# RWKV layer, tree feed-forward, attention and mixture of experts in one kernel: one product of the rwkv chunk moved from VectorE to ScalarE and GpSimd, with a new order of work

## The chip, the cores and the metric

The kernel runs on one core of a Trainium2 chip. The metric is the device time in microseconds (us). The engines are named as the profile names them: PE (TensorE matmuls, PEld its weight loads), DVE (VectorE), ACT (ScalarE), POOL (GpSimd) and SP (SyncE, which only issues transfers here).

## The reference

Sixteen sequences of 512 positions with 128 features pass through two layers. Each step is followed by a layer normalization of the input plus the step's result. Cut to what matters:

```
x = ln(x + rwkv_block(x))      # layer 0, attention place
x = ln(x + tree_ffn(x))        # layer 0, feed-forward: 8 levels of gates, 256 leaves
x = ln(x + rope_attention(x))  # layer 1: 16 heads of 8, causal softmax
x = ln(x + moe(x))             # layer 1: 16 experts, the 2 best gated, 2 shared

# inside rwkv_block, after two norms and the mixes with the shifted input:
k = exp(min(xk @ Wk, 60)); v = xv @ Wv; r = xr @ Wr; kv = k * v
# over time, for each of 512 channels:  wk_t = first*k_t + s_t,  s_{t+1} = k_t + decay*s_t
#                                       wkv_t = first*kv_t + u_t, u_{t+1} = kv_t + decay*u_t
rwkv = sigmoid(r) * (wkv / (wk + 1e-8))
x = x + rwkv @ Wo
# channel mix:
kv = silu(xk @ cWk) @ cWv
x = x + sigmoid(xr @ cWr) + kv
```

The kernel writes sigmoid(r) as (1 + tanh(r/2)) / 2, with the half in the weights. So each rwkv chunk contains a product with 1 + t, where t = tanh(r/2). The silu of the channel mix is likewise ph * (1 + tanh(ph/2)), up to the same half.

## The kernel before

**A planner at build time.** The kernel is written as Python generators ("pieces"), one for each strand of work. The class `Plan` (L66) runs them on modelled engine times while the program is built, and so decides in which order each engine's instructions are issued. On the chip each engine runs its own list strictly in this order; semaphores do the rest. A piece that wants an engine which is busy in the plan queues for it, and the queue is ordered by the time of asking plus the piece's *slack* for that engine. The slacks are the dictionaries `S_FRONT`, `S_RWKV`, `S_GREATEST`, `S_WEIGHTED`, `S_SUMS`, `S_ENDS`, `S_GATE` and `S_EXPERTS` (L46 and on): a smaller number goes first. All instructions pass through the helper class `Engine` (L209), so nearly every row of the profile carries the line L219, and rows are told apart by their tiles.

**The pieces.** For each of the 16 sequences (`b`) there is a `front` (L547): two norms, the mixes `xk`, `xr`, `xv`, four rwkv chunks of 128 channels (`rwkv(c)`, L597), the channel mix with four `hidden(c)` (L666), the tree (`gates`, `lp`), and the queries and keys with rotary positions, split into three bf16 parts each (`parts`, L779) and sent to DRAM (`there`). A front starts when the one before has summed its rwkv product (`p<-rw`), the one before that has passed its channel mix, and the plan's clock has reached PERIOD * b - LEAD. Beside the fronts run pieces that loop over all sequences: `operands` (loads of `qop`, `kop`), `greatest` (scores `sc` and their maxima `nmx`), `weighted` (scores `st` and their exponentials `ew`), `sums` (`o`), `ends` (output of the attention, norm, `u`), `gating` (`gaug`, the gates broadcast through DRAM into `gb`), `by_gate` (`us` = `u` times a gate, on POOL) and `experts` (`acc`, sixteen matmuls on the `us`). So about three sequences are in work at once.

**Slots.** PSUM has eight banks (`BANKS`) that all matmul results share; `SCORES` says how many of them score tiles may hold at once. Two rwkv chunks may be open at a time (`chunks`), two tiles `t` of the channel mix (`halves`), three `us`.

**The rwkv chunk.** Per chunk, 128 x 512 each: DVE clamps `pk` to `k`; ACT takes exp in place and t = tanh(pr/2); DVE makes `kv`; ACT makes `fk` = first*k + eps; DVE scans `sk` and then `skv`; POOL adds `fk` to `sk`. Then

```python
            W.scalar_tensor_tensor(skv, kv, first[:, c:c + 1], skv, ALU.mult, ALU.add)
            W.scalar_tensor_tensor(skv, t, 1.0, skv, ALU.add, ALU.mult)
            yield
            V.reciprocal(sk, sk)
            yield
            G.tensor_tensor(rw[:, c, :], skv, sk, ALU.mult)
```

`V` and `W` are DVE (`W` with a plan cost that counts a busy POOL), `G` is POOL, `act` is ACT, `mm` is PE.

Of the kernel before, what the change touches and what calls it, by code (L numbers as in the profile page):

```python
# [11 lines left out]
AF = mybir.ActivationFunctionType  # L12
ALU = mybir.AluOpType
# [26 lines left out]

HAND_OVER = 0.2
BANKS = 8
SCORES = 4
PERIOD = 107.0

S_FRONT = {"PE": -6.0, "V": -6.0, "A": 0.0, "G": 10.0}  # L46
S_RWKV = {"PE": -10.0, "V": 15.0, "A": 10.0, "G": 6.0}
S_GREATEST = {"PE": -15.0, "V": -6.0, "A": -6.0, "G": 20.0}
S_WEIGHTED = {"PE": -3.0, "A": -6.0}
S_SUMS = {"PE": 6.0}  # L50
S_ENDS = {"PE": 3.0, "V": -3.0, "A": 30.0, "G": 50.0}
S_GATE = {"V": 6.0, "G": 15.0}
S_EXPERTS = {"PE": 20.0}
FREE = {}
LEAD = 60.0
RWKV_PACE = 5.0
EXPERT_PACE = 0.0
MAX_PACE = 0.0
EXP_PACE = 0.0
# [198 lines left out]
def rwkv_tree_attn_moe(ctx: ExitStack, tc: tile.TileContext, a: dict, out: bass.AP):  # L258
# [16 lines left out]
    plan, table = Plan(tc), [None]  # L275

    def scalar_us(op, out, x, f=None, *_):
        us, wanted = 0.2 + 0.00078 * columns(out), {AF.Ln: "ln", AF.Tanh: "tanh"}.get(f, table[0])
        if wanted != table[0]:
# [4 lines left out]
    mm, tr, act, copy = (Engine(plan, "PE", nc.tensor, tensor_us).matmul, Engine(plan, "PE", nc.tensor, tensor_us).transpose,  # L284
                         Engine(plan, "A", nc.scalar, scalar_us).activation, Engine(plan, "A", nc.scalar, scalar_us).copy)
# [5 lines left out]
    W = Engine(plan, "V", nc.vector, beside)  # L291
    V, G = Engine(plan, "V", nc.vector, vector_us), Engine(plan, "G", nc.gpsimd, pool_us)
    banks, scores, chunks, sets = Banks(plan, BANKS), Slots(plan, SCORES), Slots(plan, 2), Slots(plan, OPERANDS)
    e_slots, us_slots, gb_slots = Slots(plan, 2), Slots(plan, 3), Slots(plan, 2)
    halves, norms = Slots(plan, 2), Slots(plan, 1)
    shifts = Slots(plan, 1)
    held, happened = {}, {}

    def event(*key):
        return happened.setdefault(key, Event(plan))  # L300
# [12 lines left out]
    def fixed(name, shape, dtype=F32):  # L313
        return const.tile(shape, dtype, tag=name, name=name)
# [27 lines left out]

    V.memset(mean_w, 1.0 / D)
    V.tensor_tensor(centre, ident, mean_w, ALU.subtract)
    eps = fixed("eps", [128, 4])
    V.memset(eps[:, 0:1], LN_EPS)
    V.memset(eps[:, 1:2], RMS_EPS)
    V.memset(eps[:, 2:3], K_EPS)

    V.memset(eps[:, 3:4], LN_EPS * RMS_EPS)  # L350
    ln_eps, rms_eps, k_eps, z_eps = (eps[:, i:i + 1] for i in range(4))

    def centred(w, scale):

# [147 lines left out]
    def bank(name, shape=(128, 512), dtype=F32):  # L502
        i = yield banks
        p = ps.tile(list(shape), dtype, tag=f"b{i}", name=name)
        held[id(p)] = p, i
        return p

    def give(p):
        banks.put(held.pop(id(p))[1])
# [3 lines left out]
    def t512(tag):  # L513
        return (p2 if tag in twice else pp).tile([128, T], F32, tag=tag, name=tag)
# [32 lines left out]
    def front(b, keep):  # L547

        if b:
            yield event("summed", b - 1)  # L550
            if b > 1:
                yield event("mixed", b - 2)
            yield max(0.0, PERIOD * b - LEAD - plan.now)
        sq, rr = f"sq{b % 2}", f"r{b % 2}"
# [42 lines left out]
        def rwkv(c):  # L597
            chunk = yield chunks
            cs = slice(c * 128, (c + 1) * 128)
            pk = yield from bank("pk")  # L600
            mm(pk, tm_k[:, cs], xk, start=True, stop=True)
            yield
            k = t512(f"k{chunk}")
            V.tensor_scalar(k, pk, K_CLAMP, None, ALU.min)
            give(pk)
            pr = yield from bank("pr")
            mm(pr, tm_r[:, cs], xr, start=True, stop=True)
            yield
            act(k, k, AF.Exp)
            t = t512(f"t{chunk}")  # L610
            act(t, pr, AF.Tanh, scale=0.5)
            give(pr)
            pv = yield from bank("pvv")
            mm(pv, tm_v[:, cs], xv, start=True, stop=True)
            yield
            kv = t512(f"kv{chunk}")
            V.tensor_tensor(kv, k, pv, ALU.mult)
            give(pv)
            fk = t512(f"fk{chunk}")
            act(fk, k, AF.Identity, bias=k_eps, scale=first[:, c:c + 1])  # L620
            dec = decay[:, c:c + 1].to_broadcast([128, T - 1])
            sk = t512(f"sk{chunk}")
            skv = t512(f"skv{chunk}")
            G.memset(sk[:, 0:1], 0.0)
            G.memset(skv[:, 0:1], 0.0)
            W.tensor_tensor_scan(sk[:, 1:T], dec, k[:, 0:T - 1], 0.0, ALU.mult, ALU.add)
            yield
            G.tensor_tensor(sk, fk, sk, ALU.add)
            W.tensor_tensor_scan(skv[:, 1:T], dec, kv[:, 0:T - 1], 0.0, ALU.mult, ALU.add)

            W.scalar_tensor_tensor(skv, kv, first[:, c:c + 1], skv, ALU.mult, ALU.add)
            W.scalar_tensor_tensor(skv, t, 1.0, skv, ALU.add, ALU.mult)
            yield
            V.reciprocal(sk, sk)
            yield
            G.tensor_tensor(rw[:, c, :], skv, sk, ALU.mult)
            chunks.put(chunk)
            event("rw", b, c).set()

        for c in range(NC4):  # L640
            plan.start(plan.now + RWKV_PACE * c, rwkv(c), S_RWKV)
        yield event("outputs")
# [21 lines left out]
        hid = pp.tile([128, NC4, T], F32, tag="four", name="hid")  # L664

        def hidden(c):  # L666
            ph = yield from bank("ph")
            mm(ph, cm_k[:, c * 128:(c + 1) * 128], xk, start=True, stop=True)
            yield
            slot = yield halves  # L670
            t = t512(f"t{slot}")
            act(t, ph, AF.Tanh, scale=0.5)
            yield
            V.scalar_tensor_tensor(hid[:, c, :], t, 1.0, ph, ALU.add, ALU.mult)
            give(ph)
            halves.put(slot)
            event("hid", b, c).set()

        for c in range(NC4):
            plan.start(plan.now + 1.2 * c, hidden(c), S_FRONT)  # L680
        pr = yield from bank("pr2")
        mm(pr, cm_r, xr, start=True, stop=True)
        yield
        t = xr
# [91 lines left out]
            G.tensor_tensor(rot[:, i, :], rot[:, i, :], rs, ALU.add)  # L776
        event("rot", b).set()
        yield
        parts = pp.tile([128, PARTS, 2, T], BF16, tag="parts", name="parts")  # L779
        copy(parts[:, 0], rot)  # L780
        yield
# [10 lines left out]
        there = dram.tile([2, PARTS, 128, T], BF16, tag="there", name="there")  # L792
        for n in range(2):
            nc.sync.dma_start(out=there[n].rearrange("a p t -> p a t"), in_=parts[:, :, n, :])
        keep["z"], keep["xa"], keep["there"] = z, xa, there
        yield 4.0
        event("there", b).set()
# [67 lines left out]
    def values(b, keep):  # L865
        if b:
            yield event("o", b - 1, NG - 1)
        pv = yield from bank("pvt")
        for t in range(NT):
            mm(pv[:, t * 128:(t + 1) * 128], keep["xa"][:, t * 128:(t + 1) * 128], w_qkv[:, 4, :], start=True, stop=True)  # L870
        yield
        copy(vheads[:, :, :, 0:DH], pv.rearrange("p (t h d) -> p t h d", t=NT, d=DH))
        give(pv)
        event("values", b).set()

    def weighted():

        for b in range(B):
            for g in range(NG):
                yield event("max", b, g)  # L880
                if g == 0:
                    plan.start(plan.now, values(b, kept[b]), S_ENDS)
                n, qo, ko = kept[b]["ops", g]
# [174 lines left out]
    def experts():  # L1058

        for b in range(B):  # L1060
# [13 lines left out]
            yield  # L1074
            plan.start(plan.now, output(b, acc), S_ENDS)

    def output(b, acc):
        slot = yield norms
        r = yield from normed(acc, "sqb", "rb")
        V.tensor_tensor(r, r, acc, ALU.mult)  # L1080
        give(acc)
        event("out", b).set()
        yield
        pt = yield from bank("pout")
        for t in range(NT):
            tr(pt[:, t * 128:(t + 1) * 128], r[:, t * 128:(t + 1) * 128], ident)
        yield
        o = t512("sqb")
        copy(o, pt)
        give(pt)  # L1090
        nc.sync.dma_start(out=out[b].rearrange("(t p) d -> p t d", p=128), in_=o.rearrange("p (t d) -> p t d", d=D))
        norms.put(slot)

    kept = {b: {} for b in range(B)}
    for b in range(B):
        plan.start(0.0, front(b, kept[b]), S_FRONT)
    for piece, slack in ((prepare_mixes, FREE), (prepare_tree, FREE), (prepare_attention, FREE), (prepare_experts, FREE), (operands, FREE),
                         (greatest, S_GREATEST), (weighted, S_WEIGHTED), (sums, S_SUMS), (ends, S_ENDS), (gating, S_ENDS),
                         (by_gate, S_GATE), (experts, S_EXPERTS)):
        plan.start(0.0, piece(), slack)  # L1100
# [54 lines left out]
```

## Time and profile before

| what | us |
|---|---|
| median of 3 runs | 1921.01 (1915.64 to 1925.85) |
| the profiled execution, its own time | 1919.29 |
| its span on the engines | 1917.5 |

Busy in that span: PE 1710.9 us, DVE 1515.0, ACT 1073.4, POOL 833.9. A row of the profile's groups gives line, engine, operation, tiles as out<-in, shapes, number, busy us and mean ns, and then the idle time just before these instructions with what ended it. A row of a tile's view gives min/median/max ns in place of the mean. "The chain of waits" follows the work that ended last back to its start, and shares the span out among what it passes through.

The first `xk` of the sequences begin at 24, 98, 182 and 271 us, and from there to the sixteenth at 1595 us once in 110.3 us.

### The profile page before, as it was taken

The numbers are of one execution on the slowest core, as the hardware profiler recorded it, in microseconds if no ns is written. First come the engines' busy times: TensorE is split into PE (matmuls) and PEld (weight loads), VectorE is DVE, ScalarE is ACT, GpSimd is POOL, SyncE is SP. The second block draws the span as 40 slices with busy tenths as digits, with TensorE's granted clock in tenths as the row PEclk, the third lists the DMA queues.
The fourth block names the chain that finished last, engine by engine and source line by source line (L and its number), as shares of the span: only waits on it lengthen the run. The fifth ranks groups of instructions, "written<-read, shape, count | busy, mean of one in ns | idle before, by whom it ended". The sixth has DMA issues, their size and how long they took to land.

```text
span 1917.5 us, 25366 instructions
## 1 busy us (share of the span) xinstructions
PE 1710.9 (89%) x8659; PEld 795.3 (41%) x8750; DVE 1515.0 (79%) x2255; ACT 1073.4 (56%) x1806; POOL 833.9 (43%) x963
## 2 busy tenths in 40 slices
PE   5556799999999999999999998989999999999995
PEld 2122344444444444444444444434444444444442
DVE  7595989797797979788887979969797988966433
ACT  3334567556466565656666564746556466565541
POOL 1223233543353546354553544436454454535353
PEclk8687999999999999999999999999999999999998
DMA  3001011312213122121312222122222212133333
GB/s 99 1 6 54 19 44 31 98 52 60 81 41 98 65 81 81 56 89 38 114 54 82 79 78 82 41 75 70 85 71 82 73 62 84 44 88 105 112 115 101
DMA packets 61969, 133.78 MB, mean 70 GB/s; under 512 B 11708, under 2 KB 32974, under 8 KB 61585
## 3 DMA queue, kind: packets, MB, share of 16 engines
q1 hardware_dynamic: 61841, 132.16, 22.3%
q8 instruction: 70, 1.15, 0.2%
q14 instruction: 58, 0.48, 0.1%
HBM read 114.01 MB, written 17.31 MB: 68 GB/s over the span
## 4 chain that ended last, share of the span: by engine, by line
PE 48%; DVE 35%; POOL 5%; DMA 4%; issue 4%; ACT 3%; SPq 1%; DVEq 0%; POOLq 0%; ACTq 0%
DVE skv L219 9%; DVE sk L219 7%; PE acc L219 6%; PE sc L219 6%; PE p L219 6%; PE st L219 5%; DVE nmx L219 5%; PE o L219 4%; DVE lp L219 4%; PE pv L219 3%; PE pr L219 3%; PE ph L219 2%; PE pvv L219 2%; DMA gb<-gd 2%; POOL us L219 2%
## 5 line engine op out<-in xcount | busy, mean ns | idle before, releaser
L219 ACT ACTIVATE ew<-st 128x512 f32<-128x512 f32 (+1 forms) x704 | 382.9, 557 | 345.2 <-PE st L219 342.3
L219 DVE TENSOR_REDUCE nmx<-sc 128x1 f32<-128x384 f32 (+3 forms) x704 | 435.4, 632 | 147.8 <-PE sc L219 108.8
L219 POOL TENSOR_TENSOR us<-u,gb 128x512 f32<-128x512 f32 x248 | 347.9, 1414 | 285.5 <-PE acc L219 181.1
L219 PE MATMUL acc<-us,w_mo 128*128 128x512 f32 x512 | 273.9, 623 | 11.7 <-POOL us L219 11.1
L219 PE MATMUL st<-qop,kop 128*128 128x512 bf16 x1022 | 251.9, 301 | 18.9 <-DVE att L219 6.2
L219 PE MATMUL sc<-kop,qop 128*128 128x128 bf16 (+1 forms) x1018 | 254.0, 302 | 12.1 <-DVE nmx L219 4.3
L219 DVE RECIPROCAL sk<-sk 128x512 f32<-128x512 f32 x64 | 213.7, 3341 | 0.0
L219 PE MATMUL o<-ew,vaug 128*32 128x512 f32 (+3 forms) x2048 | 193.5, 444 | 3.5 <-ACT ew L219 0.8
L219 POOL TENSOR_TENSOR sk<-fk,sk 128x512 f32<-128x512 f32 x64 | 100.3, 1567 | 217.5 <-DVE sk L219 149.6
L219 PEld LDWEIGHTS <-qop 128*128 128x128 bf16 x1024 | 92.0, 99 | 204.7 <-issue 185.1
L219 POOL TENSOR_TENSOR rw<-skv,sk 128x512 f32<-128x512 f32 x64 | 84.1, 1314 | 192.7 <-DVE sk L219 192.7
L219 PE MATMUL st<-idents,masks 128*128 128x128 bf16 (+2 forms) x672 | 159.7, 238 | 0.1
L219 PE MATMUL sc<-masks,idents 128*128 128x128 bf16 (+2 forms) x653 | 153.0, 234 | 0.5 <-issue 0.3
L219 PEld LDWEIGHTS <-kop 128*128 128x128 bf16 x1024 | 91.0, 98 | 149.5 <-issue 118.3
L219 DVE TENSOR_TENSOR_SCAN skv<-decay,kv 128x511 f32<-128x511 f32 x64 | 117.2, 1832 | 0.0
L219 PEld LDWEIGHTS <-idents 128*128 128x128 bf16 x704 | 69.4, 99 | 91.7 <-issue 85.9
L219 PE MATMUL p<-rw,w_tm 128*128 128x512 f32 x128 | 73.6, 658 | 37.8 <-POOL rw L219 30.9
L219 PEld LDWEIGHTS acc<-us,w_mo 128*128 128x128 f32 x512 | 80.9, 193 | 60.6 <-issue 23.0
L219 PE MATMUL pv<-sq,mean_w 128*128 128x512 f32 x160 | 91.7, 656 | 11.8 <-ACT sq L219 10.1
L219 DVE SCALAR_TENSOR_TENSOR lp<-gates,lp 128x8 f32<-128x8 f32 (+6 forms) x224 | 100.4, 489 | 0.5
L219 PEld LDWEIGHTS <-masks 128*128 128x128 bf16 x704 | 69.1, 98 | 69.9 <-issue 65.1
L219 ACT ACTIVATE r<-pv,eps 128x512 f32<-128x512 f32 x96 | 66.0, 688 | 56.9 <-PE pv L219 31.7
(200 smaller groups left out, 3023.8 us busy)
## 6 DMA issues: line engine op xcount, KB each, us to landing
gb<-gd SPq DMA_DIRECT2D x128, 512.0 KB
qop<-there SPq DMA_DIRECT2D x576, 32.0 KB
kop<-there SPq DMA_DIRECT2D x192, 96.0 KB
there<-parts SPq DMA_DIRECT2D x32, 384.0 KB
x<-xT SPq DMA_DIRECT2D x16, 256.0 KB
out<-sqb SPq DMA_DIRECT2D x16, 256.0 KB
qop<-rows SPq DMA_DIRECT2D x192, 4.0 KB
w_mo<-w_mo SPq DMA_DIRECT2D x1, 1160.0 KB
```

The lines of the kernel that those rows point to most:

```text
L219: ins = getattr(self.engine, op)(out, *args, **kw)
```

## The change

- The product with 1 + t: after the tanh, ACT adds one to `t` in place (an Identity activation with a column `one` of the small tile `eps` as bias), and POOL multiplies `skv` by it. DVE's second scalar_tensor_tensor of the chunk goes.
- The channel mix: ACT writes the tanh into `hid` itself, and DVE's product works in place there. The tiles `t` of the channel mix and their two slots (`halves`) go.
- The piece `front` waits, before it makes its `parts`, until the transfers of the `parts` of the sequence before have been issued in the plan (event `sent`).
- `SCORES` 4 to 6, `PERIOD` 107 to 104, `RWKV_PACE` 5 to 3, and nearly all slacks have other values. With them the order on every engine is another.

By the instruction lists of the two programs, DVE has 64 instructions of 128 x 512 fewer (and a memset of one column more), ACT 64 more, POOL 64 more; PE and SP issue the same ones in another order. ACT's list has 98 loads of an activation table before, 74 after.

```diff
-SCORES = 4
-PERIOD = 107.0
-
-S_FRONT = {"PE": -6.0, "V": -6.0, "A": 0.0, "G": 10.0}
-S_RWKV = {"PE": -10.0, "V": 15.0, "A": 10.0, "G": 6.0}
-S_GREATEST = {"PE": -15.0, "V": -6.0, "A": -6.0, "G": 20.0}
-S_WEIGHTED = {"PE": -3.0, "A": -6.0}
+SCORES = 6
+PERIOD = 104.0
+
+S_FRONT = {"PE": -3.0, "V": -6.0, "A": 30.0, "G": 20.0}
+S_RWKV = {"PE": -10.0, "V": 6.0, "A": 6.0, "G": 10.0}
+S_GREATEST = {"PE": -30.0, "V": -3.0, "A": -10.0, "G": -30.0}
+S_WEIGHTED = {"PE": -20.0, "A": 15.0, "G": -20.0}
 S_SUMS = {"PE": 6.0}
-S_ENDS = {"PE": 3.0, "V": -3.0, "A": 30.0, "G": 50.0}
-S_GATE = {"V": 6.0, "G": 15.0}
-S_EXPERTS = {"PE": 20.0}
+S_ENDS = {"PE": 3.0, "V": -3.0, "A": -30.0, "G": 30.0}
+S_GATE = {"PE": 0.0, "V": 0.0, "A": 6.0, "G": 50.0}
+S_EXPERTS = {"PE": 50.0}
 FREE = {}
 LEAD = 60.0
-RWKV_PACE = 5.0
+RWKV_PACE = 3.0
...
             mm(pv, tm_v[:, cs], xv, start=True, stop=True)
             yield
+            act(t, t, AF.Identity, bias=one)
             kv = t512(f"kv{chunk}")
...
             W.scalar_tensor_tensor(skv, kv, first[:, c:c + 1], skv, ALU.mult, ALU.add)
-            W.scalar_tensor_tensor(skv, t, 1.0, skv, ALU.add, ALU.mult)
+            G.tensor_tensor(skv, t, skv, ALU.mult)
             yield
             V.reciprocal(sk, sk)
...
-            slot = yield halves
-            t = t512(f"t{slot}")
-            act(t, ph, AF.Tanh, scale=0.5)
-            yield
-            V.scalar_tensor_tensor(hid[:, c, :], t, 1.0, ph, ALU.add, ALU.mult)
+            act(hid[:, c, :], ph, AF.Tanh, scale=0.5)
+            yield
+            V.scalar_tensor_tensor(hid[:, c, :], hid[:, c, :], 1.0, ph, ALU.add, ALU.mult)
             give(ph)
-            halves.put(slot)
...
+        if b:
+            yield event("sent", b - 1)
         parts = pp.tile([128, PARTS, 2, T], BF16, tag="parts", name="parts")
...
             nc.sync.dma_start(out=there[n].rearrange("a p t -> p a t"), in_=parts[:, :, n, :])
+        event("sent", b).set()
```

More of the change, by code (lines that the diff above doesn't have):

```diff
@@ L294, in rwkv_tree_attn_moe @@
     e_slots, us_slots, gb_slots = Slots(plan, 2), Slots(plan, 3), Slots(plan, 2)
-    halves, norms = Slots(plan, 2), Slots(plan, 1)
+    norms = Slots(plan, 1)
     shifts = Slots(plan, 1)
@@ L344, in rwkv_tree_attn_moe @@
     V.tensor_tensor(centre, ident, mean_w, ALU.subtract)
-    eps = fixed("eps", [128, 4])
+    eps = fixed("eps", [128, 5])
+    V.memset(eps[:, 4:5], 1.0)
     V.memset(eps[:, 0:1], LN_EPS)
@@ L350, in rwkv_tree_attn_moe @@
     V.memset(eps[:, 3:4], LN_EPS * RMS_EPS)
-    ln_eps, rms_eps, k_eps, z_eps = (eps[:, i:i + 1] for i in range(4))
+    ln_eps, rms_eps, k_eps, z_eps, one = (eps[:, i:i + 1] for i in range(5))
     def centred(w, scale):
```

## The prediction

> **What bounds the kernel now.** I read the page's busy table and slices first, then a table by stage, then the chain of waits, and last the tiles that the change touches. The busy table and the slices of PE and DVE:
>
> ```profile
> span 1917.5 us, 25366 instructions
> PE 1710.9 (89%) x8659; PEld 795.3 (41%) x8750; DVE 1515.0 (79%) x2255; ACT 1073.4 (56%) x1806; POOL 833.9 (43%) x963
> ...
> PE   5556799999999999999999998989999999999995
> ...
> DVE  7595989797797979788887979969797988966433
> ```
>
> PE is near its limit from slice 5 on, and DVE is the second busiest. The same by stage (columns: stretch, its length, busy us of PE, PEld, DVE, ACT, POOL, then TensorE clock and DMA):
>
> ```profile
> 0.00:200.00 200.00, 116.98 (x228) 47.18 (x230) 141.53 (x212) 72.98 (x112) 49.08 (x64) 0.77 0.12 38
> 200.00:900.00 700.00, 648.53 (x3385) 304.91 (x3418) 594.17 (x855) 426.22 (x710) 308.64 (x371) 0.99 0.21 64
> 900.00:1600.00 700.00, 659.89 (x3412) 307.91 (x3448) 590.72 (x864) 415.79 (x705) 336.32 (x379) 0.99 0.24 74
> 1600.00:1850.00 250.00, 238.90 (x1501) 116.70 (x1518) 171.16 (x294) 146.03 (x260) 110.86 (x130) 1.00 0.29 86
> ```
>
> PE idles 83 us of the first 200, then 51.5 and 40.1 us of two stretches of 700, then 11 of 250. So after the start at most some 100 us can be won on PE at all. DVE idles 106 and 109 us in the two long stretches: it isn't full, but it is what the end hangs on, after PE:
>
> ```profile
> PE 48%; DVE 35%; POOL 5%; DMA 4%; issue 4%; ACT 3%; SPq 1%; DVEq 0%; POOLq 0%; ACTq 0%
> DVE skv L219 9%; DVE sk L219 7%; PE acc L219 6%; PE sc L219 6%; PE p L219 6%; PE st L219 5%; DVE nmx L219 5%; PE o L219 4%; DVE lp L219 4%; PE pv L219 3%; PE pr L219 3%; PE ph L219 2%; PE pvv L219 2%; DMA gb<-gd 2%; POOL us L219 2%
> ```
>
> The largest entry, DVE on `skv`, is where the change cuts. Its three instructions per chunk, with POOL's reading of them (min/median/max ns):
>
> ```profile
> L219 DVE TENSOR_TENSOR_SCAN skv<-decay,kv x64: 1195/2012/2287, 30.9 to 1651.2; 128x511 f32<-128x511 f32 x64
> L219 DVE SCALAR_TENSOR_TENSOR skv<-kv,first,skv x64: 750/1494/1820, 32.2 to 1653.0; 128x512 f32<-128x512 f32 x64
> L219 DVE SCALAR_TENSOR_TENSOR skv<-t,skv x64: 691/693/1594, 33.8 to 1654.6; 128x512 f32<-128x512 f32 x64
> L219 POOL TENSOR_TENSOR rw<-skv,sk x64: 1260/1270/2138, 38.1 to 1661.8; 128x512 f32<-128x512 f32 x64
> ```
>
> **What the Trainium skill says.** "ScalarE: Activation LUTs", What ACT_TABLE_LOAD costs: an ACTIVATE with a pointer bias takes 280 ns + 0.833 ns per element, 706 ns for 512; the trace has 718 for `xx<-xn,vec`, the same operation. A table load is put at 1283 ns, and the trace has 1283. Its section Table sets says that identity stands in every set, so the new ACTIVATE should load none. "GPSIMD Engine Reference", Engine selection, puts a two-input elementwise operation at about twice VectorE's time; 1270 against 693 ns above agrees. Its Specifications say that GpSimd shares its SBUF interfaces with VectorE and contends with instructions of two SBUF inputs; the spread from 750 to 1820 ns of one and the same STT agrees.
>
> **The change, part by part.**
> (a) *DVE loses `skv<-t,skv`*: 64 x 0.933 us (its mean in the groups by form) = 59.7 us, 3.73 us a sequence. The three `skv` rows sum to 117.2 + 78.4 + 59.7 = 255.3 us, and the chain holds 8.7% of 1917.5 = 167 us of them, 65%. So 0.65 x 3.73 = 2.4 us a sequence come off the chain.
> (b) *ACT gains `t<-t,eps`*: 64 x 0.718 = 46 us, straight after the tanh that makes `t`. Against it the instruction lists have 74 table loads where there were 98: 24 x 1.283 = 31 us less. ACT is busy 56% and 3% of the chain, so +15 us costs nothing while `t` is ready before DVE's scans (1.42 + 1.83 us) are through. Without that cover it costs at most 0.718 us a chunk on POOL.
> (c) *POOL gains `skv<-t,skv`*: between 64 x 1.31 (row `rw`) = 84 us and 64 x 1.57 (row `sk<-fk,sk`) = 100 us; I take 84. In the list it always follows `sk<-fk,sk`. That one starts at the end of DVE's first scan and takes 1.57; DVE needs 1.83 + 1.23 = 3.06 until `skv` is there. So POOL also stands still for 1.49 us, 95 us in all, with whatever is behind it: `us` in 23 of 64 places, the next chunk's `sk<-fk,sk` in 17, `rw` in 15. The chain itself does not grow: DVE goes on to the reciprocal (3.34 us) and POOL needs 1.31 beside it before `rw` can start. If POOL is late, `rw` is late, then PE's `p<-rw`.
> (d) *Contention*: POOL stands still during the second STT now, where 37 of 64 `sk<-fk,sk` were followed at once by `us`. If the STT falls from its mean of 1225 to 750 ns, that is 30 us of DVE; the displaced `us` and the new product stretch other DVE instructions. Bounds +15 and -30 us of DVE; I take 0.
> (e) *tanh in place*: the same ACT and DVE instructions on another tile (0.595 and 0.685 us); the limit of two `t` tiles goes. DVE waits 52.4 us for that tanh in 39 places, off PE's path; from 0 to -10 us, I take 0.
> (f) *parts wait for `sent`*: the wait on the transfer is in the program before already (the copy reuses one buffer); its transfer left a period earlier. Now the planner knows of it. 0; if the transfers of two sequences before were late, `four` would be held and the next `hid` with it, up to 1 us a sequence.
> (g) *Slacks, PERIOD, SCORES* change no work, only the order. At the 16th sequence's first `pk`, 279.5 us of pure multiply time (columns by the back-to-back rate, 0.86 us for 512 of fp32) remain on PE, against 263.5: fronts go in sooner. Changes between fp32, bf16 and 32-column matmuls fall from 2021 to 1915 of 6534. From the two long stretches, an order can cost PE 5.7% to 7.4% of idle; over 1324 us that is 22 us either way. I take 0.
>
> **The sum.** *Start* (to 271 us, where the fourth sequence's `pk` can begin): sequences follow one another through DVE here, so three of them save 3 x 3.73 = 11; I take -10 for handovers. PE's waits there are the sign:
>
> ```profile
> PE p L219 <- POOL rw L219: 29.7, 4, 11.2
> ```
>
> *Steady part* (271 to 1595, twelve periods of 110.3): PE idles 1324 - 1242.3 = 81.7, 6.8 a period. (a) gives 12 x 2.4 = -29; a PE idle of 4.4 a period would be left. *Tail* (1595 to the end, 322 us): no `skv` in most of it; 16 us more multiply time is merely moved; the list leaves one sequence's experts (8 `us`) after the last `u` on POOL instead of 12, so 4 x 1.27 = 5 us that overlap in part: -2. Sum -41: from the profiled execution's own 1919.3 us (span 1917.5 + 1.8) to 1878. The median of the runs is 1.7 above that execution, so 1880.
>
> **The rivals.**
> 1. *More*: (d) at its good end (-20 on the chain at 65%) and fewer changes of kind on PE (106 x some 0.1 us = -10): 1850. For it: the STT's spread. Against: contention moves rather than goes.
> 2. *PE is the bound, DVE was hidden*: PE is 94% busy in the steady part, and its 7% idle comes back under other names (`pmx` on POOL, `gaug`). Only half of the start is won, -5: 1916.
> 3. *Slower, POOL's queue*: the 84 us of work and 95 us of standing still bring POOL from 834 to 1013 us, and the blocked `us` reach PE, which takes them in order. 23 places x (1.49 + 1.31) = 64 us against -41: +23, so 1944. Against it: POOL waits 181.1 us for PE's `acc` before `us`, so it is ahead, and three `us` buffers cover three of PE's 6.9 us steps (110.3 / 16), 20 us. It decides only if POOL falls behind by more than these 20 us.
>
> **How the numbers follow.** The sum as worked out 0.55, more 0.17, hidden 0.14, POOL's queue 0.14. A measurement of this kernel tells 0.5%, some 10 us, from no change. Faster 0.55 + 0.17 = 0.72, same 0.14, slower 0.14. Range: 1845 takes in the first rival with (e); 1930 takes in the second and the bad end of (g) (1880 + 22) and of (f) (+16), and leaves the core of the third out.
>
> **What would show it.** Right: DVE near 1455 us without the row `skv<-t,skv`; ACT near 1088 with 74 loads; a POOL row `skv<-t,skv` of about 1.3 us with some 95 us of idle ahead of it put to DVE `skv`; `skv` under 7% of the chain; PE idle in the middle near 5%; the first x of the 16th sequence some 35 us before 1581. Wrong: `acc` waiting for POOL `us` by tens of us more than now; PE idle of the middle unchanged; periods of 110 us or more; `p<-rw` late.

## The result and the profile after

| what | us |
|---|---|
| before, median of 4 runs | 1921.68 (1915.64 to 1925.85) |
| changed, median of 4 runs | 1899.95 (1891.05 to 1904.40) |
| ratio, with its 95% interval | 0.9884 (0.9839 to 0.9928) |
| changed, the profiled execution's own time | 1899.65 |

The kernel became 1.2% faster, by some 22 us. The forecast was 1880, so the direction held and about half of the gain of 41 us came. First the busy table, the slices of PE and DVE, and the chain of waits of the changed kernel:

```profile
span 1897.9 us, 25479 instructions
PE 1719.6 (91%) x8750; PEld 800.3 (42%) x8750; DVE 1453.8 (77%) x2192; ACT 1086.3 (57%) x1846; POOL 893.1 (47%) x1027
...
PE   5556799999999999999999999999999999999995
...
DVE  7695969797788889787898879787878879655422
...
PE 55%; DVE 24%; POOL 6%; issue 5%; DMA 4%; ACT 3%; SPq 2%; POOLq 0%; DVEq 0%; ACTq 0%
PE acc L219 8%; PE sc L219 8%; PE p L219 8%; PE st L219 7%; DVE sk L219 6%; PE o L219 5%; DVE skv L219 5%; PE pv L219 4%; DVE nmx L219 3%; PE pr L219 2%; PE pk L219 2%; POOL us L219 2%; PE ph L219 2%; DVE lp L219 2%; DMA gb<-gd 2%
```

DVE has lost 61 us of work, `skv` has gone from the head of the chain to 5%, and the chain runs over PE instead. The table by stage says where PE's idle time went (columns as before: stretch, length, busy us of PE, PEld, DVE, ACT, POOL, clock, DMA):

```profile
0.00:200.00 200.00, 123.53 (x237) 50.44 (x238) 146.99 (x205) 79.13 (x123) 59.16 (x77) 0.78 0.12 38
200.00:900.00 700.00, 657.14 (x3492) 309.78 (x3491) 575.07 (x856) 432.40 (x736) 340.35 (x401) 0.98 0.21 67
900.00:1600.00 700.00, 672.50 (x3505) 313.35 (x3503) 587.07 (x846) 437.31 (x744) 367.07 (x416) 0.99 0.23 72
1600.00:1850.00 250.00, 238.31 (x1467) 115.97 (x1467) 132.42 (x259) 132.31 (x235) 115.05 (x128) 0.98 0.30 96
```

PE idles 76.5, 42.9, 27.5 and 11.7 us, where it idled 83, 51.5, 40.1 and 11.1. Part of the difference is only in the records: the profile before has 8659 of PE's 8750 matmuls, this one has all. By an estimate (the weight loads that stand without a matmul get one of 512 columns) the lost records are worth 2.7 and 2.9 us of the two long stretches, so PE idled about 49 and 37 us there. The work moved as worked out. This is the scalar_tensor_tensor that DVE keeps in the rwkv chunk (min/median/max ns), and then come the two new instructions in the groups (busy us and mean ns, then the idle time ahead of them and what ended it):

```profile
L219 DVE SCALAR_TENSOR_TENSOR skv<-kv,first,skv x64: 750/752/1512, 34.0 to 1595.4; 128x512 f32<-128x512 f32 x64
```

```profile
L219 ACT ACTIVATE t<-t,eps 128x512 f32<-128x512 f32 x64 | 46.2, 721 | 0.8
L219 POOL TENSOR_TENSOR skv<-t,skv 128x512 f32<-128x512 f32 x64 | 89.3, 1396 | 107.5 <-DVE skv L219 104.4 <-ACT gates L219 3.1
```

POOL stands still for 104 us in front of the product, as the price of taking its list in order. Whether that reaches anyone is read from the waits (us in all, times, longest):

```profile
DVE nmx L219 <- PE sc L219: 176.1, 215, 5.9
...
PE p L219 <- POOL rw L219: 44.1, 10, 8.6
...
PE acc L219 <- POOL us L219: 13.5, 8, 4.5
```

The same waits before, with one more that stands ahead of `p` (it is put to POOL's memset of `skv`, but these matmuls read `rw`):

```profile
DVE nmx L219 <- PE sc L219: 108.8, 157, 7.6
...
PE p L219 <- POOL rw L219: 30.9, 8, 11.2
...
PE acc L219 <- POOL us L219: 11.1, 10, 5.8
...
PE p L219 <- POOL skv L219: 6.7, 2, 5.3
```

DVE now waits for PE's scores much longer than it did, so it follows PE more than before. PE stands 44.1 us ahead of `p<-rw`, where it stood 37.8 (all causes), so some 6 us longer, and hardly longer ahead of `acc<-us`.

### The profile page after: what moved, and what is told of

The parts are those of the page before. It is cut to its first block, busy times and chain, and to the rows that moved or that the text cites. A ratio compares the mean times of both kernels' runs of the same rounds, so it can differ in the third digit from the quotient of the medians.

```text
span 1897.9 us, 25479 instructions
## 1 busy us (share of the span) xinstructions
PE 1719.6 (91%) x8750; PEld 800.3 (42%) x8750; DVE 1453.8 (77%) x2192; ACT 1086.3 (57%) x1846; POOL 893.1 (47%) x1027
## 4 chain that ended last, share of the span: by engine, by line
PE 55%; DVE 24%; POOL 6%; issue 5%; DMA 4%; ACT 3%; SPq 2%; POOLq 0%; DVEq 0%; ACTq 0%
PE acc L219 8%; PE sc L219 8%; PE p L219 8%; PE st L219 7%; DVE sk L219 6%; PE o L219 5%; DVE skv L219 5%; PE pv L219 4%; DVE nmx L219 3%; PE pr L219 2%; PE pk L219 2%; POOL us L219 2%; PE ph L219 2%; DVE lp L219 2%; DMA gb<-gd 2%
## 5 line engine op out<-in xcount | busy, mean ns | idle before, releaser
L219 POOL TENSOR_TENSOR us<-u,gb 128x512 f32<-128x512 f32 x248 | 329.5, 1340 | 216.0 <-PE acc L219 147.2
L219 PE MATMUL acc<-us,w_mo 128*128 128x512 f32 x512 | 273.5, 628 | 13.5 <-POOL us L219 13.5
L219 PE MATMUL st<-qop,kop 128*128 128x512 bf16 (+3 forms) x1024 | 255.2, 302 | 26.5 <-DMA qop<-rows 17.6
L219 PE MATMUL sc<-kop,qop 128*128 128x128 bf16 (+3 forms) x1024 | 257.5, 304 | 7.6 <-DVE nmx L219 4.0
L219 PE MATMUL o<-ew,vaug 128*32 128x512 f32 (+3 forms) x2048 | 188.7, 446 | 3.2 <-DVE nmx L219 1.7
L219 PE MATMUL sc<-masks,idents 128*128 128x128 bf16 (+2 forms) x704 | 173.6, 247 | 0.0
L219 PE MATMUL st<-idents,masks 128*128 128x128 bf16 (+2 forms) x704 | 172.1, 244 | 0.0
L219 POOL TENSOR_TENSOR sk<-fk,sk 128x512 f32<-128x512 f32 x64 | 95.9, 1498 | 155.6 <-DVE sk L219 113.8
L219 POOL TENSOR_TENSOR skv<-t,skv 128x512 f32<-128x512 f32 x64 | 89.3, 1396 | 107.5 <-DVE skv L219 104.4
L219 PE MATMUL p<-rw,w_tm 128*128 128x512 f32 x128 | 75.9, 677 | 44.1 <-POOL rw L219 44.1
L219 DVE TENSOR_TENSOR_SCAN skv<-decay,kv 128x511 f32<-128x511 f32 x64 | 104.6, 1634 | 0.0
L219 DVE TENSOR_TENSOR_SCAN sk<-decay,k 128x511 f32<-128x511 f32 x64 | 104.4, 1631 | 0.0
```

What stands on the lines that cost most here:

```text
L219: ins = getattr(self.engine, op)(out, *args, **kw)
```

## The experiments

Two helpers recur. In a **frozen list** the planner is told the cost that the edited instruction had in the kernel whose order is kept. The new instruction is then issued outside the plan, so that every other instruction keeps its place on every engine:

```diff
+    def unplanned(name, issue, *args, **kw):
+        with tc.issue_after(plan.last[name].ins):
+            plan.last[name] = issue(*args, **kw)
```

The other way is a **new plan**: one constant is changed and the planner writes another order of the same work. Ratios are to the kernel before, run on the same chip beside each.

**1. The move in the old order** (frozen list of the kernel before; nothing else of the change):

```diff
+            unplanned("A", nc.scalar.activation, t, t, AF.Identity, bias=one)
...
-            W.scalar_tensor_tensor(skv, t, 1.0, skv, ALU.add, ALU.mult)
+            plan.did("V", beside("scalar_tensor_tensor", skv))
+            unplanned("G", nc.gpsimd.tensor_tensor, skv, t, skv, ALU.mult)
```

> The kernel before with the product alone moved to ScalarE and GpSimd; the planner is told that DVE still does it, so all other instructions keep the order of before on every engine. Theory 'the freed DVE time gives the gain': 29 us of the steady part, as in the prediction, and nothing else: 1890 to 1900, DVE near 1455 us. Rival 'the new order gives it': POOL's standing still ahead of the product (some 95 us) gives back what DVE saves, 1915 to 1925. Second rival 'POOL's queue': in an order that wasn't made for it the product comes late, us and rw with it, over 1925.

Measured: 1907.86 us (1906.02 to 1916.52), ratio 0.9936 (0.9912 to 0.9960), between the first theory and its rival. Its profile, which is of the slowest of the seven runs, 1916.52 us:

```profile
PE 1729.8 (90%) x8750; PEld 800.8 (42%) x8750; DVE 1449.7 (76%) x2192; ACT 1116.8 (58%) x1870; POOL 892.1 (47%) x1027
...
PE 64%; DVE 17%; POOL 6%; ACT 5%; DMA 4%; issue 3%; SPq 1%; POOLq 0%; DVEq 0%; ACTq 0%
```

DVE sheds 65 us and falls from 35% of the chain to 17%, yet the time falls by 0.64% only, 12 us (by the two medians 16). What DVE gives up on the chain, PE takes (48% before, 64% here). The `xk` of the second to fourth sequences begin at 95, 182 and 272 us, and before at 98, 182 and 271: the start gains nothing. Nor do the twelve periods after it in this execution: 110.4 us each, as before.

**2. The new order without the move** (frozen list of the changed kernel, the product on DVE again):

```diff
-            act(t, t, AF.Identity, bias=one)
+            plan.did("A", scalar_us("activation", t, t, AF.Identity))
...
-            G.tensor_tensor(skv, t, skv, ALU.mult)
+            plan.did("G", pool_us("tensor_tensor", skv))
+            unplanned("V", nc.vector.scalar_tensor_tensor, skv, t, 1.0, skv, ALU.add, ALU.mult)
```

> The changed kernel with the product back on DVE; the planner is told that it is on ScalarE and GpSimd, so all other instructions keep the changed kernel's order. Theory 'freed DVE time': 1915 to 1925, as before, with DVE near 1515 us. Rival 'new order': 1895 to 1905, as the changed kernel. If the two add up, this and the move in the old order together make the 22 us.

Measured: 1937.46 us (1935.88 to 1941.78), ratio 1.0090 (1.0065 to 1.0115), above both theories. The order by itself is slower than the old one. Within this order the move is worth 0.9884 / 1.0090 = 0.980, some 37 us, two to three times what it is in the old order. Added up, the two halves would give 0.9936 x 1.0090 = 1.0025; together they give 0.9884. So the gain is not the sum of a move and an order: the move is worth more in the order that was written for it.

The three traces show where. These are the twelve periods from the fourth `xk` to the sixteenth, in the kernel before, in this run and in the changed kernel (columns as in the table by stage):

```profile
270.80:1595.30 1324.50, 1242.81 (x6457) 581.87 (x6524) 1118.47 (x1624) 798.04 (x1340) 615.87 (x705) 0.99 0.23 71
```

```profile
278.90:1583.60 1304.70, 1228.12 (x6463) 577.29 (x6462) 1086.91 (x1608) 764.86 (x1304) 598.65 (x694) 0.98 0.23 70
```

```profile
277.80:1548.50 1270.70, 1218.78 (x6463) 572.68 (x6462) 1052.77 (x1561) 793.97 (x1352) 647.02 (x743) 0.99 0.23 72
```

The second and the third have the same order, and here the move takes off 34 us. What is left after the sixteenth `xk` takes 351 us in this run and 349 in the changed kernel, and the stage before the fourth 279 and 278. So nearly all that the move is worth in this order, it is worth in the middle.

**3. The move planned with the old constants** (new plan; the changed kernel with the slacks, `PERIOD` 107, `SCORES` 4 and `RWKV_PACE` 5 of before, and the channel mix as before):

```diff
-SCORES = 6
-PERIOD = 104.0
+SCORES = 4
+PERIOD = 107.0
...
-S_RWKV = {"PE": -10.0, "V": 6.0, "A": 6.0, "G": 10.0}
+S_RWKV = {"PE": -10.0, "V": 15.0, "A": 10.0, "G": 6.0}
...
-RWKV_PACE = 3.0
+RWKV_PACE = 5.0
```

> The kernel before with the product moved and the planner told so, and the wait for 'sent'; SCORES, PERIOD, slacks and the tanh of the channel mix as before. Theory 'freed DVE time': 1890 to 1905, like the move in the old order. Rival 'new constants are needed': 1910 to 1925. A difference of more than 10 us from the move in the old order would be the worth of one order against another.

Measured: 1956.64 us (1952.63 to 1962.97), ratio 1.0189 (1.0160 to 1.0218). The same move, planned by the constants that suited the kernel before, is 1.9% slower than no move, and slower than either theory had it. PE waits 23.3 us for `us` and 50.5 for `rw`.

**4. and 5. Neighbouring orders of the changed kernel** (new plans; `HAND_OVER` is what the plan allows between two steps of a piece):

```diff
-HAND_OVER = 0.2
+HAND_OVER = 0.19
```

> The changed kernel planned with a hand-over of 0.19 us between two steps of a piece instead of 0.2: no work changes, only the order that comes out. If orders made from the same constants are worth the same, 1895 to 1905; if one order among many was chosen for its time, 1905 to 1930, and the spread says how much of any difference is the order.

Measured: 1925.62 us (1918.92 to 1932.88), ratio 1.0016 (1.0004 to 1.0029).

```diff
-HAND_OVER = 0.2
+HAND_OVER = 0.22
```

> The changed kernel planned with a hand-over of 0.22 us: the same work in another order. A second draw beside that of 0.19 us. If the order of the changed kernel is a lucky or a chosen one: 1910 to 1940. If 0.19 was the unlucky one: 1895 to 1905.

Measured: 1925.28 us (1920.72 to 1931.97), ratio 1.0025 (1.0015 to 1.0035). Both do the same work as the changed kernel in another order, and lose its whole gain. So the changed kernel's order is a good one among many; no neighbour of the order before was run, so how good a pick that one is stays unknown. In the first, PE idles 49.2 and 39.0 us of the two long stretches:

```profile
200.00:900.00 700.00, 650.79 (x3416) 306.42 (x3415) 562.33 (x844) 423.98 (x723) 332.27 (x393) 0.98 0.21 64
900.00:1600.00 700.00, 660.99 (x3491) 308.59 (x3489) 566.93 (x826) 430.70 (x736) 353.55 (x408) 0.99 0.23 71
```

and PE waits for POOL's `us` 29.0 us in place of the changed kernel's 13.5, the sign that the third rival named:

```profile
PE acc L219 <- POOL us L219: 29.0, 14, 7.1
```

In the second that wait is 35.2 us, yet its twelve periods take 105.8 us each, as little as the changed kernel's; it lies behind after the sixteenth `xk`, with 382 us in place of 349.

**6. and 7. Two more plans.**

```diff
-SCORES = 6
+SCORES = 5
```

> The changed kernel with five banks for scores instead of six, planned anew. Theory 'an order is a draw': 1905 to 1940 with no relation to the number of banks. Rival 'the sixth bank is what decouples PE from DVE's maxima': PE waits for nmx grow by 20 us or more and the time is over 1925.

Measured: 1899.62 us (1898.16 to 1902.07), ratio 0.9890 (0.9864 to 0.9915). The lists of all engines came out the same as the changed kernel's (in the traces too, the records of DVE, ACT, POOL and PEld stand in the same order), so the sixth bank plays no part in this order. The run stands as a repeat of the changed kernel, and agrees with it.

```diff
-PERIOD = 104.0
+PERIOD = 107.0
```

> The changed kernel planned with the old PERIOD of 107: fronts may not start as soon, and the order is another. Theory 'an order is a draw': 1900 to 1935 with PE's wait for us telling where in it. Rival 'the shorter period is what gains': 1925 to 1940, with a period of 109 us or more on the chip.

Measured: 1936.52 us (1929.40 to 1938.27), ratio 1.0077 (1.0061 to 1.0092). PE waits 29.9 us for `us`. The periods are 109.0 us, and the time lies in the rival's range, just above that of "an order is a draw". So the shorter `PERIOD` may well be part of the gain; the fifth experiment shows that it isn't enough.

**8. and 9. A fourth `us` buffer**, in the changed kernel's order and in that of `HAND_OVER` 0.19. The buffers change and the lists stay; two small tiles of the setup share other tiles' room to make space:

```diff
-    p3 = ctx.enter_context(tc.tile_pool(name="p3", bufs=3))
+    p3 = ctx.enter_context(tc.tile_pool(name="p3", bufs=4))
...
-        b0r = pp.tile([PARTS, D], F32, tag="b0r", name="b0r")
+        b0r = pp.tile([PARTS, D], F32, tag="gT", name="b0r")
...
-        b0m = pp.tile([PARTS, D], BF16, tag="b0m", name="b0m")
+        b0m = pp.tile([PARTS, D], BF16, tag="rb", name="b0m")
```

> The changed kernel in its own order with four buffers for us in memory instead of three (the planner still counts three, two small setup tiles share the room of others). POOL waits 147 us for PE's acc before us, with the rest of its queue behind it, and PE waits 13.5 us for us. Theory 'POOL's queue is a small cost in this order': 1890 to 1900, the wait of POOL for acc well under 147 us. Rival 'no cost at all': 1898 to 1903. Rival 'us made earlier collide with DVE's two-input instructions': over 1905.

> The kernel planned with a hand-over of 0.19 us (1925.6 us), its order kept, with the same fourth buffer for us. There PE waits 29 us for us, against 13.5 in the changed kernel. Theory 'the slower orders are slow by POOL's queue': the wait falls by 10 us or more and the time to 1905 to 1918. Rival 'they are slow by something else': 1922 to 1928.

Measured: 1903.09 us (1900.47 to 1904.37), ratio 0.9907 (0.9894 to 0.9920), and 1922.14 us (1916.27 to 1926.59), ratio 1.0011 (0.9999 to 1.0023). In the changed kernel's order POOL's wait for PE before `us` falls from 147.2 to 42.6 us:

```profile
POOL us L219 <- PE acc L219: 42.6, 14, 15.5
```

and no time follows. In the other order PE's wait for `us` stays at 28.1 us. So the late `us` are not late for want of a buffer. What stands ahead of them in POOL's list is left, and the tenth experiment takes that up.

**10. The other order without POOL's product** (the list of the fourth experiment; only the `skv<-t,skv` of POOL is left out, so the rwkv result lacks its gate):

```diff
-            G.tensor_tensor(skv, t, skv, ALU.mult)
+            plan.did("G", pool_us("tensor_tensor", skv))
```

> The kernel planned with a hand-over of 0.19 us (1925.6 us), its order kept, with POOL's product skv with 1 + t left out, so the factor is missing from rwkv. POOL loses 87 us of work and 108 us of standing still. Theory 'in the slower orders the product in POOL's queue makes us late for PE': PE's wait for us falls from 29 us to 15 or less and the time to 1900 to 1912. Rival 'the slower orders are slow by how PE's own work falls, not by POOL': PE's wait for us falls by less than 8 us and the time stays at 1918 to 1926.

Measured: 1903.16 us (1898.88 to 1906.08), ratio 0.9876 (0.9853 to 0.9898), 22 us less than the fourth experiment (27 by the two ratios). PE idles 40.1 and 32.9 us of the long stretches:

```profile
200.00:900.00 700.00, 659.91 (x3493) 309.29 (x3494) 570.49 (x848) 434.54 (x741) 313.30 (x379) 0.98 0.22 68
900.00:1600.00 700.00, 667.11 (x3478) 312.16 (x3476) 571.86 (x826) 429.82 (x734) 327.58 (x379) 0.98 0.24 72
```

```profile
PE acc L219 <- POOL us L219: 18.8, 10, 7.2
```

The wait for `us` falls by 10 us, between what the two theories put it at, and `p<-rw` from 47.0 to 41.0. So in this order the product in POOL's list costs about 22 us: the third rival's mechanism, at work, though these two waits hold only 16 of them. The matching run, the changed kernel's own order without the product, was not made. That the product costs less there is argued from the wait of 13.5 us, and from the periods: without the product they fall from 107.4 to 106.1 us here, and the changed kernel has 105.9 with it.

**11. The tanh in place alone** (the kernel before with only that edit, its slots kept so that the order stays):

```diff
-            t = t512(f"t{slot}")
-            act(t, ph, AF.Tanh, scale=0.5)
+            act(hid[:, c, :], ph, AF.Tanh, scale=0.5)
             yield
-            V.scalar_tensor_tensor(hid[:, c, :], t, 1.0, ph, ALU.add, ALU.mult)
+            V.scalar_tensor_tensor(hid[:, c, :], hid[:, c, :], 1.0, ph, ALU.add, ALU.mult)
```

> The kernel before with the tanh of the channel mix written into hid, everything else and every order as before. DVE waited 52.4 us for that tanh in 39 places, off PE's path. Theory 'the edit itself costs and gains nothing': 1916 to 1928. Rival 'the shared tiles t held the front up': 1905 to 1915, and DVE's wait for the tanh falls by more than 20 us.

Measured: 1922.07 us (1915.55 to 1928.16), ratio 1.0007 (0.9996 to 1.0017). DVE's wait for that tanh stays at 51.4 us in 38 places (52.4 before). Its fall to 19.8 us in the changed kernel comes from the order, and the edit itself is worth nothing.

**12. The reciprocal left out** (frozen list of the changed kernel; a product with zero stands in its place, so the rwkv result is zero):

```diff
-            V.reciprocal(sk, sk)
+            plan.did("V", vector_us("reciprocal", sk))
+            unplanned("V", nc.vector.tensor_scalar, sk, sk, 0.0, None, ALU.mult)
```

> The changed kernel in its own order with the reciprocal of the rwkv chunk left out (a product with zero of the same tile takes its place, so rwkv is zero): some 64 x 2.9 = 186 us of DVE go. Theory 'PE is next': DVE still held the changed kernel by part of PE's 170 us of idle; with DVE near 1270 us the start (72 us of idle) and some of the middle shrink: 1855 to 1880. Rival 'DVE still is the bound': far more, under 1840. Rival 'PE and its clock alone': 1890 to 1900.

Measured: 1874.32 us (1870.99 to 1880.02), ratio 0.9762 (0.9735 to 0.9788). The busy table and the chain:

```profile
PE 1715.4 (91%) x8671; PEld 802.6 (43%) x8750; DVE 1283.1 (68%) x2192; ACT 1085.5 (58%) x1846; POOL 894.7 (48%) x1027
...
PE 64%; DVE 15%; POOL 6%; issue 5%; DMA 4%; ACT 3%; SPq 2%; POOLq 0%; DVEq 0%; ACTq 0%
```

DVE loses another 171 us, nearly three times what the change took off it, and the time falls by some 25. The start gives most of it: the fourth `xk` begins at 256 us in place of 278. The twelve periods after it take 1272.7 us, and 1270.6 in the changed kernel, so there nothing is left to win on DVE, and the chain lies on PE.

## Why the prediction was right in direction and wrong in size

**The sum by its stages.** From profile to profile the time fell by 1919.29 - 1899.65 = 19.6 us, where the sum had 41:

| stage | predicted | measured | from |
|---|---|---|---|
| start | -10 | about +2 | fourth `xk` at 278 in place of 271; 4.7 us more multiply time is done by then, worth 5.4 at the steady pace of 0.870 |
| steady | -29 | about -30 | see below |
| tail | -2 | about +8 | 349 us in place of 322, with 16 us more multiply time, worth 19.6 at the old tail's pace of 0.818 |

*Steady, right, with luck in the number.* Between the fourth and the sixteenth `pk` the kernel before did 1151.5 us of pure multiply time in 1324 us (0.870), the changed one 1130.8 in 1270 (0.890). At equal work that is 1130.8 x (1324/1151.5 - 1270/1130.8) = 30 us. The period fell from 110.3 to 105.9, PE's idle time in the two long stretches to 70.4 of 1400 ("near 5%"), and the first x of the sixteenth sequence came at 1532 in place of 1581, sooner than the 35 us named; the order has part in this, for without the move it stands at 1567. The mechanism, freed DVE time, is shown by the second experiment: in the new order the move takes 34 us off the twelve periods. That the number agrees so closely is luck. The step reckoned with the old order, and there the periods did not shrink (110.4 us in the first experiment's profile) and the whole gain was some 12 us. Also, repeats of the changed kernel's list differ by up to 6 us in this stage (1270.6, 1274.0 and 1276.8 us).

*Start, the first step that failed.* "Three of them save 3 x 3.73 = 11" took the rwkv chunks as one strand through DVE. In the changed kernel the last `rw` of the third sequence did come 12 us earlier (at 235 in place of 247), but by the runs the move has little of this: in the old order it brings 1 us (246), and the new order without the move stands at 239. Two reasons show. Of DVE's time only some 60% is on the path there: leaving out the reciprocal took 36 us off DVE's work up to the fourth `xk` (207.8 to 171.5), and the fourth began 22 earlier. And POOL's product takes some back: without it the third `rw` of the fourth experiment's order comes at 230 in place of 234. The sign named for the start, PE's wait for `rw`, rose in the first 200 us from 29.7 to 39.4 us (35.0 to 39.4 with all waits ahead of `p<-rw`):

```profile
PE p L219 <- POOL rw L219: 39.4, 6, 8.6
```

Then the new order spends what was won: the fourth `xk` comes 43 us after that last `rw` in place of 24, with or without the move (40 in the second experiment).

*Tail, the second.* That the multiply time is "merely moved" nearly held: 16 us cost 18.4 at the middle's pace of 0.870 and 19.6 at the tail's. What the sum had at nothing is the pace itself, which fell to 0.800 (279.5 us of multiply time in 349). This is the order's doing, for without the move the tail takes 351 us. By the granted clock TensorE loses 19.7 us from 1600 us on, and 6.2 before; some of it falls where PE idles, so how much of the 8 us this makes stays open.

**The edits.** (a) DVE at 1453.8 us, against 1455; `skv` on the chain 4.9%, against "under 7%". (b) ACT at 1086.3, against 1088. POOL's product waited for DVE, and hardly for ACT. (c) The product took 1396 ns in the mean, 89 us, within 84 to 100, and POOL stood still 104 us for it, against 95. (d) Contention at 0 nearly held in sum, though nothing stayed in place: the STT (scalar_tensor_tensor) fell from 1225 to 992 ns in the mean (15 us in 64) and the scan into `skv` from 1832 to 1634 (13), while the scan into `sk` rose from 1423 to 1631 (13) and the five mixes by some 19 together. (e) was 0, as the eleventh experiment shows. (f) No run has it alone; PE's wait for `qop<-rows` rose from 3.7 to 17.6 us, but it is 4.3 in the third experiment, which has the `sent` wait under the old constants; so it came with the new order, and what the `sent` wait does in that order stays open.

**(g), the order, is the step that was mis-sized.** "22 us either way, I take 0" bounded it from the idle shares of two stretches of one trace. The runs show far more. Six orders of the same moved work took 1900 (the changed kernel's), 1908 (the old list), 1925, 1926, 1937 and 1957 us. The spread is 57 us. Four of the six are slower than the kernel before (two of them by 0.2% only), and three of these four were planned with the new constants and one number changed. So neither the move nor the new constants make the gain by themselves; this one order does.

**The rivals.** *More* had little part that shows: contention moved, and what fewer changes of kind on PE bring was not measured. *PE is the bound* was half true: some of PE's idle time did come back under other names (6 us ahead of `p<-rw`, 14 at `qop<-rows`), and the twelfth experiment shows that DVE is spent as a source in the middle, but the change still won its 30 us there. *POOL's queue* did not decide here by its own sign, since `acc<-us` rose by 2.4 us only. What the product costs in the changed kernel's order was not measured, and in a neighbouring order it is 22 us. Its point of decision was misplaced: the cover of three buffers does not decide, since a fourth changed nothing in either order. What is left is where the `us` stand in POOL's list relative to the product, which the tenth experiment supports and does not prove.

## What to carry to other kernels

When work moves between engines that run fixed lists, predict the move and the order together, and give the order a range as wide as the spread of several orders of the same work, not as the idle share of one trace. Time taken off an engine counts by the share of it that is on the path in that stage: here some 60% at the start. Before moving work onto an engine with a queue, look at who sits behind the place where it will stand still; one buffer more did not help here.

## What the runs showed of the hardware

TensorE's granted clock falls to half for slices of 3.4 us, or a multiple, after short idle gaps, even in stretches where PE is 94% busy (for instance from 640.0 to 643.4 us in the changed kernel). Between 200 and 1800 us of the changed kernel, the 3.4 us ahead of such a slice hold 1.1 to 3.0 us of PE idle time. In sum the withheld clock comes to 66 us in the kernel before and 85 us in the changed one, two thirds and half of them in the first 200; where PE idles anyway, this costs no time. The Trainium skill's "TensorE: Matmul & The Clock Gate", Part 1: The HAM clock gate, describes these two states and a window of 3.4 us, and the slices agree. What was not expected is that the times of the runs go with it: over 28 runs of the kernel before, whose mean clocks lie from 0.960 to 0.969, each 0.001 of clock goes with 1.4 us (correlation -0.73). The changed kernel's runs lie at 0.955 to 0.960. By that slope its lower clock, some 0.007, would cost about 10 us of its gain; this is an estimate from the slope, which doesn't say what causes what, and no run isolates it.
